# Batch 29 of a graph layer: exponentials kept in the PSUM banks of the distances, and masked from there

## Chip, core and metric

The kernel runs on one core of a Trainium2 chip. The metric is the device time of one execution in microseconds (us), and the time of a kernel is the median over several executions. A profile is one further execution, recorded instruction by instruction. Its span runs from the first to the last instruction. Engines are named as in the profile: PE (TensorE, matrix products), PEld (its weight loads), DVE (VectorE), ACT (ScalarE), POOL (GpSimd) and SP (SyncE, which issues most transfers here).

## What is computed

The input is `x` (32 batches of 512 nodes with 256 features, fp32) and `adj` (32 masks of 512 x 512, fp32 zeros and ones). After a layer norm and a relu, which give the `x` below, the layer computes for each batch:

```python
xc = transpose(x)
h = relu(bn1(conv1(xc)));  h = bn2(conv2(h, 17 taps))
x_conv = transpose(relu(h + xc))
s = x @ w_se.T + b_se                    # 3 numbers per node
sq = sum(s * s, axis=-1)
dist = sq[:, :, None] + sq[:, None, :] - 2.0 * einsum('bnd,bmd->bnm', s, s)
A = exp(-dist) * mask                    # 512 x 512 for each batch
msg = relu(x @ w_msg.T + b_msg)
x_nmp = einsum('bnm,bmd->bnd', A, msg)
# then a gated unit on [x_conv, x_nmp] and x; its output is added to the input
```

The change touches the line that forms `A`, for one batch of the 32.

## The kernel before

**Stages.** The 32 batches are worked in two groups of 16 (`GB`). For each group, `first_part` normalises, runs conv1 and takes the data to a frequency form, in which conv2 is a set of small products. Then `nodes` runs over the 16 batches of the group; it does the frequency products (`product`) and, batch by batch, distances, exponentials, mask and the sum over neighbours. After both groups a last phase goes through the 16 pairs of batches: `inverse` takes conv2 back, `gates_rz` and `gate_n` form the gates, `finish` stores the result. Every phase issues its instructions in an order written out by hand; each engine works through its own in that order and waits only for semaphores.

**The node loop.** For group 1 the order of batches is 31, 30, 16, 17, ..., 29, so batch 29 = `B - 3` is the last one. The loop works one batch ahead: while it sums batch `b` over its neighbours, it prepares the next, `more[0]`. The steps for a batch are

- `factors` (L467): two transposes on PE of the small feature tables give `SL` and `SR`;
- `turn` (L479): DVE turns 128 x 512 pieces of the mask into the tile `at`, of which there are two buffers;
- `exponents` (L486): four products `pd` (L493) put the negated distances of 128 nodes against 512 into four PSUM banks, then four ACTIVATEs on ACT (L495) write their exponentials into the SBUF tile `A` (two buffers);
- `masked` (L497): DVE multiplies each quarter of `A` by its piece of the mask (L499), in place;
- `aggregate` (L526) or, for most batches, `aggregate7` (L538): PE sums over the neighbours.

`aggregate` makes two results of 128 x 512 (L532), one for each half of the 256 features. Each is a chain of four products, over the four quarters of `A` in order. A product in fp32 shows in the trace as two MATMUL instructions, so a result is eight of them. ACT copies each result out of its bank (L534), and `save_nmp` (L571) stores both halves.

**The end of the second loop.** With `last` = 13, the 15th and the 16th batch (28 and 29) go through `aggregate`, and there are no frequency products left to put between. The order on PE is then: first half of batch 28, the distances of batch 29, second half of batch 28, both halves of batch 29. On DVE it is: `turn` of the quarters 0 and 1, `masked` of 0 and 1, `turn` of 2 and 3, `masked` of 2 and 3.

**What comes next.** The last phase starts on other engines before this is over. POOL loads the operands of the first pair and the combined weights, and forms the differences that the gates need (`sums`, L649; L653 in the trace, on the tiles `hp`, `np`, `cp`), four for each tile. PE goes on with `inverse` of pair 0 (L663, banks `pc`), whose result DVE and ACT turn into `cp` (L667, L669), and then the gates (`into`, L675).

**Banks.** There are eight PSUM banks, and all that needs one takes the next in turn: `bank(name)` (L105) asks a pool with eight buffers and one tag. A bank asked for comes free when everything that reads its earlier tenant is done.

Of the kernel before, what the change touches and what calls it, by code (L numbers as in the profile page):

```python
# [12 lines left out]
AF = mybir.ActivationFunctionType  # L13
# [52 lines left out]
def gnn_layer(  # L66
# [15 lines left out]
    nc = tc.nc  # L82
    B, N, D = x.shape
# [21 lines left out]
    def bank(name):  # L105
        return psum.tile([P, N], FP, tag="bank", name=name)

    X, ADJ, XN, HT, HQ, H1, MSG, A, NMP, ST, SL, SR = ({} for _ in range(12))
    XP, HP, NP, CP, YT, RZ, NT, OUT, AT, TS, MS = ({} for _ in range(11))
# [376 lines left out]
    def exponents(b):  # L486

        A[b] = pools["nodes"].tile([P, NC, N], FP, tag="A", name=f"A_{b}", bufs=2)
        sl, sr = SL.pop(b), SR.pop(b)
        pd = [bank(f"pd_{b}_{mc}") for mc in range(NC)]  # L490
        for mc in range(NC):
            rows = slice(32 * mc, 32 * mc + 3 * NS)
            nc.tensor.matmul(pd[mc], sl[rows, :], sr[rows, :], start=True, stop=True)  # L493
        for mc in range(NC):
            nc.scalar.activation(A[b][:, mc, :], pd[mc], AF.Exp)  # L495

    def masked(b, mcs):  # L497
        for mc in mcs:
            nc.vector.tensor_mul(A[b][:, mc, :], A[b][:, mc, :], AT.pop((b, mc)))  # L499

    H = N // 2

    def quads(t, width):
        return [t[:, 2 * k : 2 * k + 2, width * j : width * (j + 1)] for k in range(2) for j in range(2)]

    def affinity_sums(b):
        b11, b12, b21, b22 = quads(A[b], H)
        t = TS[b] = pools["seven"].tile([P, 3, 2, H], FP, tag="ts", name=f"ts_{b}", bufs=1)
        sub = ALU.subtract
        return [partial(nc.gpsimd.tensor_tensor, dst, x, y, op=sub)  # L510
                for dst, x, y in ((t[:, 0], b22, b12), (b12, b12, b11), (t[:, 1], b22, b12), (t[:, 2], b21, t[:, 1]))]
# [26 lines left out]
    def aggregate7(b):  # L538

        m11, s1, m12, m22 = quads(MSG.pop(b), P)  # L540
        b11, t1, b21, b22 = quads(A.pop(b), H)
        (s3, s2, s4), (t3, t2, t4) = ([t[:, n] for n in range(3)] for t in (MS.pop(b), TS.pop(b)))
        nmp = NMP[b] = work.tile([P, DC, N], FP, tag="nmp", name=f"nmp_{b}", bufs=1)
        c11, c12, c21, c22 = (nmp[:, i, H * j : H * (j + 1)] for i in range(2) for j in range(2))
        p1 = pools["seven"].tile([P, H], FP, tag="p7", name=f"p7_{b}", bufs=3)

        def add_product(bk, left, right, first):
            for k in range(2):
                nc.tensor.matmul(bk, left[:, k, :], right[:, k, :], start=(first and k == 0), stop=(k == 1),  # L549
                                 skip_group_check=True)  # L550

        x, y, z = (bank(f"pn{k}_{b}")[:, :H] for k in range(3))
        add_product(x, m11, b11, True)
# [457 lines left out]
    with tc.tile_pool(name="freq", bufs=1) as fpool:  # L1011
# [33 lines left out]
        def nodes(g, xf, units, last, following=()):  # L1045
# [35 lines left out]
            message(todo[1], [1])  # L1081
            features(todo[1])
            exponents(todo[0])
            turn(todo[0], [0, 1])
            masked(todo[0], [0, 1])
            turn(todo[0], [2, 3])
            masked(todo[0], [2, 3])
            prepare(pw, g, units[1], xf)
            for step in affinity_sums(todo[0]):
                step()  # L1090
            for i, b in enumerate(todo):
# [36 lines left out]
                if more:  # L1128
                    turn(more[0], [0, 1])
                    exponents(more[0])  # L1130
                    masked(more[0], [0, 1])
# [122 lines left out]
```

## Time and profile before

| | |
|---|---|
| median of four runs | 1807.76 us (1806.5 to 1809.77) |
| the profiled execution | 1805.22 us |
| its span | 1803.1 us |
| mean granted clock of TensorE | 0.999 |

The stages in the profiled execution, with the busy time of the engines in each (us):

| from : to | length | PE | DVE | ACT | POOL |
|---|---|---|---|---|---|
| 0 : 164, first part of group 0 | 164.00 | 159.14 | 122.53 | 90.67 | 54.39 |
| 164 : 420, node loop of group 0 | 256.00 | 255.73 | 207.07 | 131.02 | 201.93 |
| 420 : 556, first part of group 1 | 136.00 | 135.93 | 107.14 | 57.94 | 60.16 |
| 556 : 808, node loop of group 1 | 252.00 | 251.82 | 193.53 | 124.85 | 193.10 |
| 808 : 823.6, its end, up to the distances of batch 29 | 15.60 | 15.60 | 10.82 | 6.85 | 8.86 |
| 823.6 : 837.7, batch 29 | 14.10 | 12.03 | 7.78 | 3.82 | 12.99 |
| 837.7 : 1803.1, inverse and gates | 965.40 | 956.54 | 564.81 | 220.54 | 258.44 |

The bounds of the stages are put by hand where the work changes. Matmuls overlap, so the busy time of PE is the time in which at least one is under way.

How to read the lines below: a line of a timeline has the start and the duration in us, the engine, the line of the kernel, the operation, the tiles (what is written <- what is read, buffer numbers left out), the size, how many instructions are merged, and in brackets the idle time of the engine before them and what ended it. A line of the chain of waits has start, duration, engine, tile, line and count: it is followed back from the last instruction, at each step to whatever released it or to the instruction before it on its engine.

### The profile page before, as it was taken

What the parts mean: (1) busy time and instruction counts of PE and PEld (TensorE: products, weight loads), DVE (VectorE), ACT (ScalarE), POOL (GpSimd) and SP (SyncE); (2) the same over time, 40 slices, a digit from 0 to 9 for tenths busy, and PEclk for the clock granted to TensorE, in tenths of its full rate; (3) what the DMA queues carried; (4) which work ended last, traced back from release to release, by engine and by line L of the source; (5) the groups of instructions that cost most, each with busy time, mean ns of one, the idle gap of its engine ahead of it and who ended that gap; (6) DMA issues with size and microseconds to landing.
All of it is one profiled execution on the core that took longest, in us unless ns stands there. A gap on an engine that the chain in (4) does not pass through costs nothing.

```text
span 1803.1 us, 21211 instructions
## 1 busy us (share of the span) xinstructions
PE 1786.8 (99%) x6974; PEld 1148.4 (64%) x6974; DVE 1213.7 (67%) x2242; ACT 635.7 (35%) x1348; POOL 789.9 (44%) x733
## 2 busy tenths in 40 slices
PE   8999999999999999999999999999999999999998
PEld 6677888888998888885554555455545554555444
DVE  7885877887986777874356645665566556655666
ACT  4556555453345445443221222122212221222121
POOL 3432887877344878786123132313321332133221
PEclk9999999999999999999999999999999999999999
DMA  9999989876769889889043234323442344124402
GB/s 257 310 300 227 244 235 237 225 214 212 236 222 232 237 227 230 237 211 313 1 123 102 46 97 123 108 48 91 123 114 52 80 123 119 59 68 123 122 19 52
DMA packets 307089, 288.27 MB, mean 160 GB/s; under 512 B 146764, under 2 KB 237420, under 8 KB 306596
## 3 DMA queue, kind: packets, MB, share of 16 engines
q1 hardware_dynamic: 296948, 261.44, 53.6%
q0 software_dynamic: 6592, 23.50, 4.2%
q10 hardware_dynamic: 3440, 1.97, 0.4%
q8 instruction: 56, 0.92, 0.2%
q14 instruction: 53, 0.43, 0.1%
HBM read 190.45 MB, written 96.40 MB: 159 GB/s over the span
## 4 chain that ended last, share of the span: by engine, by line
PE 95%; DVE 2%; issue 1%; POOL 1%; DMA 1%; ACT 0%; SPq 0%; ACTq 0%; DVEq 0%; POOLq 0%
PE pg L675 30%; PE pn L675 15%; PE py L400 12%; PE pn L549 10%; PE pm L451 6%; PE pc L336 6%; PE pc L663 5%; PE px L351 4%; PE pd L493 2%; PE pw L260 2%; PE phT L316 1%; PE pz L675 1%; PE psr L475 1%; PE pn L532 0%; DMA w2p<-in_w2T_dram 0%
## 5 line engine op out<-in xcount | busy, mean ns | idle before, releaser
L653 POOL TENSOR_TENSOR hp<-hp 128x512 f32<-128x512 f32 x64 | 81.3, 1281 | 413.2 <-DMA hp<-hd 381.8
L675 PE MATMUL pg<-hp,sw 128*128 128x512 f32 x434 | 221.8, 593 | 0.7 <-DVE rz L694 0.5
L675 PE MATMUL pg<-np,sw 128*128 128x512 f32 x434 | 221.6, 592 | 0.0
L675 PE MATMUL pg<-cp,sw 128*128 128x512 f32 x434 | 221.6, 592 | 0.0
L653 POOL TENSOR_TENSOR cp<-cp 128x512 f32<-128x512 f32 x64 | 80.6, 1269 | 229.6 <-ACT cp L669 228.4
L690 ACT ACTIVATE rz<-rz,brz 128x512 f32<-128x512 f32 x93 | 67.0, 721 | 260.2 <-DVE rz L694 260.2
L367 POOL TENSOR_TENSOR wsum<-wt 128x512 f32<-128x512 f32 x78 | 111.3, 1428 | 103.7 <-DMA wt<-wd 64.7
L400 PE MATMUL py<-wt,xf 128*128 128x256 f32 x640 | 154.2, 384 | 0.0
L675 PEld LDWEIGHTS pg<-hp,sw 128*128 128x128 f32 x434 | 82.2, 190 | 104.7 <-issue 97.1
L675 PEld LDWEIGHTS pg<-cp,sw 128*128 128x128 f32 x434 | 82.5, 190 | 103.8 <-issue 103.8
L675 PEld LDWEIGHTS pg<-np,sw 128*128 128x128 f32 x434 | 82.5, 190 | 103.8 <-issue 103.8
L499 DVE TENSOR_TENSOR A<-A,at 128x512 f32<-128x512 f32 x128 | 138.7, 1122 | 5.4 <-ACT A L495 5.2
L400 PEld LDWEIGHTS py<-wt,xf 128*128 128x128 f32 x640 | 117.1, 190 | 34.9 <-issue 19.7
L814 ACT ACTIVATE nt<-nt,vech 128x512 f32<-128x512 f32 x64 | 46.2, 722 | 236.2 <-DVE nt L813 236.2
L336 PE MATMUL pc<-w,hT 128*128 128x256 f32 x512 | 118.1, 383 | 0.8 <-DVE hT L320 0.8
L451 PE MATMUL pm<-wmsg,hq 128*128 128x259 f32 x512 | 117.5, 381 | 0.0
L675 PE MATMUL pn<-np,sw 128*128 128x512 f32 x224 | 114.4, 592 | 0.0
L675 PE MATMUL pn<-cp,sw 128*128 128x512 f32 x224 | 114.4, 592 | 0.0
L675 PE MATMUL pn<-hp,sw 128*128 128x512 f32 x224 | 114.4, 592 | 0.0
L336 PEld LDWEIGHTS pc<-w,hT 128*128 128x128 f32 x512 | 94.6, 190 | 24.2 <-issue 6.4
L451 PEld LDWEIGHTS pm<-wmsg,hq 128*128 128x128 f32 x512 | 96.5, 189 | 14.7
L663 PEld LDWEIGHTS pc<-back,yt 128*128 128x128 f32 x640 | 92.7, 190 | 7.7 <-issue 7.7
(173 smaller groups left out, 3371.8 us busy)
## 6 DMA issues: line engine op xcount, KB each, us to landing
wt<-wd SPq DMA_DIRECT2D x80, 512.0 KB, 7.4
adj<-in_adj_dram SPq DMA_DIRECT2D x128, 256.0 KB, 6.6
wd<-wst SPq DMA_DIRECT2D x64, 320.0 KB, 5.8
yd<-y SPq DMA_DIRECT2D x76, 256.0 KB, 5.2
yt<-yd SPq DMA_DIRECT2D x30, 640.0 KB, 6.5
hd<-hT SPq DMA_DIRECT2D x32, 512.0 KB, 4.9
nd<-nmp SPq DMA_DIRECT2D x32, 512.0 KB, 3.0
xb<-in_x_dram SPq DMA_DIRECT2D x128, 128.0 KB, 3.7
```

Source lines behind the costliest of these rows:

```text
L336: nc.tensor.matmul(p[:, j, :], HT[b][:, ic, c * P : (c + 1) * P], w1[:, ic, :], start=(ic == 0), stop=(ic == DC - 1))
L351: nc.tensor.matmul(p[:, j * 2 * L : (j + 1) * 2 * L], H1[b][:, c0 + j, ic * P : (ic + 1) * P], fwd, start=True, stop=True)
L367: nc.gpsimd.tensor_tensor(t, WT[g, u][:, 0], WT[g, u][:, 1], op=ALU.add)
L400: nc.tensor.matmul(dst, v[:, ic, :], w[:, ic, :], start=(ic == 0), stop=(ic == DC - 1))
L451: nc.tensor.matmul(p[:, : D + NS], hq[:, ic, c * P : (c + 1) * P], wmsg[:, ic, :], start=(ic == 0), stop=(ic == DC - 1))
L499: nc.vector.tensor_mul(A[b][:, mc, :], A[b][:, mc, :], AT.pop((b, mc)))
L549: nc.tensor.matmul(bk, left[:, k, :], right[:, k, :], start=(first and k == 0), stop=(k == 1), skip_group_check=True)
L653: nc.gpsimd.tensor_tensor(t[:, dst, :], t[:, a, :], t[:, b, :], op=sub)
L663: nc.tensor.matmul(bk[:, t0:t1], YT[p][j][:, c, oc * P : (oc + 1) * P], back[:, n : n + t1 - t0], start=(c == 0), stop=(c == len(spans) - ...
L675: nc.tensor.matmul(bk[:, t], sw[:, k, q, o, :], terms[k][q][:, t], start=(first and i == 0), stop=(i == len(ks) - 1), skip_group_check=True)
L690: nc.scalar.activation(rz[:, g, j, :], src, AF.Sigmoid, bias=brz[:, g : g + 1], scale=1.0)
L814: nc.scalar.activation(n, n, AF.Tanh, bias=b_in[:, i : i + 1], scale=1.0)
```

## The change

For the batches listed in `in_banks` the ACTIVATE writes the exponentials back into the bank that it reads, in place of a quarter of `A`; the list holds batch 29 alone. A table `EXP` keeps for each quarter where the exponentials are, and `masked` reads them from there. The product with the mask is written to `A` as before, so `aggregate` is unchanged. For all other batches the same instructions are issued as before.

```diff
@@ exponents(b)
         for mc in range(NC):
-            nc.scalar.activation(A[b][:, mc, :], pd[mc], AF.Exp)
+            if b in in_banks:
+                EXP[b, mc] = pd[mc]
+            else:
+                EXP[b, mc] = A[b][:, mc, :]
+            nc.scalar.activation(EXP[b, mc], pd[mc], AF.Exp)
 
     def masked(b, mcs):
         for mc in mcs:
-            nc.vector.tensor_mul(A[b][:, mc, :], A[b][:, mc, :], AT.pop((b, mc)))
+            nc.vector.tensor_mul(A[b][:, mc, :], EXP.pop((b, mc)), AT.pop((b, mc)))
 
     H = N // 2
+    EXP = {}
+    in_banks = (B - 3,)
```

## The prediction

> **What bounds the kernel now.** I read the page first: its busy shares and its chain.
>
> ```profile
> PE 1786.8 (99%) x6974; PEld 1148.4 (64%) x6974; DVE 1213.7 (67%) x2242; ACT 635.7 (35%) x1348; POOL 789.9 (44%) x733
> ...
> PE 95%; DVE 2%; issue 1%; POOL 1%; DMA 1%; ACT 0%; SPq 0%; ACTq 0%; DVEq 0%; POOLq 0%
> ```
>
> TensorE (PE) is at work almost throughout and is 95% of the chain that ended last. A change to four exponentials and four mask products therefore counts only where PE waits for them. So the second view is the chain of waits in the stretch from 819 to 845 us, where the last batch (batch 29) is made and used:
>
> ```profile
> 824.84 2.07 ACT A L495 x4
> ...
> 826.95 1.75 DVE A L499
> 828.70 0.68 DVE at L482 x2
> ...
> 830.42 2.84 DVE A L499
> ...
> 833.31 4.56 PE pn L532 x10
> 837.87 5.65 PE pc L663 x40
> ```
>
> Here, for once, the chain leaves PE: exponentials, masks, transposes, masks, and only then matmuls. The timeline of the same stretch gives the durations (start, duration, engine, line, count, then idle time before and what ended it):
>
> ```profile
> 823.86 5.98 POOL L653 TENSOR_TENSOR hp<-hp 128x512 f32<-128x512 f32 x4
> 824.69 5.42 PE L532 MATMUL pn<-A,msg 128*128 128x512 f32 x12
> 825.47 3.24 DVE L499 TENSOR_TENSOR A<-A,at 128x512 f32<-128x512 f32 x2 [4.09 <-ACT A L495]
> 828.63 1.29 DVE L482 STREAM_TRANSPOSE at<-adj 128x512 f32<-128x512 f32 x2
> 829.85 3.40 DVE L499 TENSOR_TENSOR A<-A,at 128x512 f32<-128x512 f32 x2
> 830.55 1.13 PE L532 MATMUL pn<-A,msg 128*128 128x512 f32 x2 [0.44 <-DVE A L499]
> 831.42 5.52 POOL L653 TENSOR_TENSOR np<-np 128x512 f32<-128x512 f32 x4
> 833.31 4.56 PE L532 MATMUL pn<-A,msg 128*128 128x512 f32 x10 [1.64 <-DVE A L499]
> 837.70 1.57 PE L663 MATMUL pc<-back,yt 128*128 128x136 f32 x10
> ```
>
> PE stands still twice, each time for a mask product. The four products take 1.56, 1.75, 0.64 and 2.83 us (starts 825.47, 826.95, 829.85, 830.42), while GpSimd (POOL) runs the subtractions of the next phase. In the whole trace only here do matmuls wait for L499.
>
> **What the two stops cost.** Matmuls of this form start 0.429 us apart (eight from 820.09 take 3.60 us; one lasts 0.592, so (3.60 - 0.592)/7 = 0.43). The group of twelve has its last start at 830.11 - 0.592 = 829.52. Twelve more follow (2 and 10), then L663. Without a stop L663 would start 13 x 0.429 = 5.58 us later, at 835.09; it starts at 837.70. The stops cost **2.61 us**: 0.60 and 1.80 of waiting, and twice 0.105 because the first matmul after each lasts 0.697.
>
> **The change, part by part.** Counts stay: four ACTIVATEs and four products for batch 29, no DMA, and nothing for the other 31 batches.
>
> *Exponentials (L495).* They read a bank as before and write the same bank, not A. No row shows ScalarE writing a bank. Successive ones start 0.48 us apart now (2.06 us for four, one is 0.594). The nearest rows on both sides: copies out of a bank (L534), 0.586, and sigmoids from SBUF to SBUF (L690), 0.722. I take 0.594, nearest because the input and the function are the same. [...]
>
> *Mask products (L499).* One input now comes from a bank. Rows with a bank first and SBUF second, in this same node loop and beside the same busy POOL:
>
> ```profile
> L454 DVE TENSOR_TENSOR msg<-pm,bmsg x128: 407/415/425, 158.0 to 812.3; 128x256 f32<-128x256 f32 x128
> ...
> L499 DVE TENSOR_TENSOR A<-A,at x128: 642/1210/2832, 167.4 to 830.4; 128x512 f32<-128x512 f32 x128
> ```
>
> (minimum, median, maximum in ns). With both inputs in SBUF the time spreads over a factor of four; with one in a bank 128 instructions stay within 18 ns. At the full width of 512 the rows with a bank are L706, 0.678 to 0.689 (two of them inside POOL's subtractions of 848.99 to 855.40), L694, 0.688, and L667, 0.751. So a product from a bank takes 0.64 (the fastest product now) to 0.75; I take 0.69, the same operation. The four fall from 6.79 to 2.76 us. [...]
>
> *New order in time.* Durations added end to end, though VectorE overlaps them a little: first product 825.47 to 826.16, second to 826.85, two transposes of 0.70 to 828.25, third to 828.94, fourth to 829.63. Undisturbed, PE asks for the first at 828.23, the second at 829.09, the third at 829.95 and the fourth at 830.80. The margins of the last two are 1.0 and 1.2 us. With every term at its upper bound (exponentials 0.72 apart, products 0.75) the third ends at 829.3 and the fourth at 830.0, still 0.7 early. Both stops go: **-2.61 us**; the product that now ends at 828.70, 0.4 ahead of its matmul, holds nothing up.
>
> *What waits move.* ScalarE no longer waits for A's old buffer; VectorE's first product does, but its last readers (the L549 matmuls) were done by 819.71, 5.8 us earlier. Behind that product stand only transposes and products of the same batch. The four banks stay taken until the products are read, some 0.7 to 3 us longer. Eight banks go round, so the next users are the second to fourth bank of the inverse and the first of the gates, the earliest at 839.1 - 2.6 = 836.5, 7 us after the last product. Cost nothing; uncovered it would be those 3 us.
>
> *What is late next.* After 837.70 PE runs on into L663 and L675. The gates' POOL operands (L653 cp) wait for ScalarE behind L663's banks, and so move along; POOL is free for them from about 837, and they start at 843.72 - 2.61 = 841.1. POOL's subtractions lose their stretches too (1.59 and 1.72 beside 1.27), about 0.8 us that stays on POOL. Transfers only start earlier. From 838 to the end the wait list names 0.7 us of PE waiting (for L694 and L706), so the gain is passed to the end. PE itself can gain no more than 2.61 + 0.7 = 3.3 us.
>
> **The sum.** The profiled execution took 1805.22 us with a span of 1803.1. Less 2.61: span 1800.5, execution 1802.6. That execution was 2.54 below the median of the four runs (1807.76; 1806.5 to 1809.77), so the forecast for the median is 1807.76 - 2.61 = **1805.15 us**, 0.14% faster. A measurement here can tell about 0.2%, 3.6 us, from no change, so the forecast counts as within it.
>
> **Rivals.**
> 1. *The products stay slow* (9%): they are long for another reason than two SBUF inputs beside POOL, and no PE time comes back: 1807.76. For it: the fourth starts 1.0 us before POOL's np subtraction. Against: L454, L706.
> 2. *Half of it* (6%): the first stop goes, 0.71 us, but the fourth product still runs into POOL and keeps its 1.90 us: 1807.05. For it: only the fourth is so long. Against: the same rows, and its start would be at 829, between POOL's two groups.
> 3. *Slower: writing into the bank being read is expensive on ScalarE* (5%). No row shows it. Up to (830.80 - 0.69 - 824.84)/4 = 1.3 us per exponential it is hidden; it decides against the change from (833.25 - 0.69 - 824.84)/4 = 1.93 us, four times today's spacing. At 3.0 us the fourth product ends at 824.84 + 12 + 0.69 = 837.5, 4.3 later than now: 1812.0.
>
> **How the numbers follow.** The likeliest, 80%, is 1805.15, by itself 1805.0 to 1805.4. The four runs lie from 1.3 below to 2.0 above their median, and a median of a few moves by about 0.9. Low end: most gain, 1807.76 - 3.3, less 0.9, about 1803.5. High end: 1807.05 of rival 2 with part of that scatter, 1807.6; beyond stay rival 3, half of rival 1 and the tails. Faster by over 0.2% (under 1804.14) needs the forecast with a favourable scatter of 1.0: 17% in all. Slower: rival 3 and a tail of rival 1: 6%. Within: 77%.
>
> **What would show it.** In the changed profile the four products read pd and at, 0.64 to 0.75 us each; L532 has no wait on L499; its matmuls after 824.69 run as one group of 24; L663 starts at 835.1; exponentials stay near 0.6 us. Products still over 1 us would prove rival 1 or 2 right, exponentials over 1.3 us rival 3. A later start of L675's first cp operand than 841.1 on POOL, or new PE waits after 838, would show a gain given back, and make the prediction wrong.

## The result, and the profile after

| | before | after |
|---|---|---|
| median | 1806.56 us (54 runs, 1804.44 to 1809.77) | 1803.12 us (36 runs, 1800.49 to 1808.25) |
| ratio, 95% interval | | 0.9982 [0.9977, 0.9987] |
| span of the profiled execution | 1803.1 us | 1801.0 us |

The change makes the kernel 0.18% faster, 3.25 us by the ratio (2.3 to 4.2 by its interval). The forecast was 0.14%, 2.61 us, and a median of 1805.15 us within 1803.5 to 1807.6. The measured median lies 0.4 us below that range.

The timeline of the profile after, in the stretch in which batch 29 is made and used (start, duration, engine, line, tiles, count, idle time before):

```profile
825.25 10.57 PE L538 MATMUL pn<-A,msg 128*128 128x512 f32 x24
835.66 0.57 PE L669 MATMUL pc<-back,yt 128*128 128x136 f32 x3
...
826.01 1.29 DVE L503 TENSOR_TENSOR A<-pd,at 128x512 f32<-128x512 f32 x2 [4.07 <-ACT pd L499]
827.22 1.30 DVE L482 STREAM_TRANSPOSE at<-adj 128x512 f32<-128x512 f32 x2
828.44 1.25 DVE L503 TENSOR_TENSOR A<-pd,at 128x512 f32<-128x512 f32 x2
...
824.41 5.21 POOL L659 TENSOR_TENSOR hp<-hp 128x512 f32<-128x512 f32 x4
829.56 1.61 POOL L623 DMA_DIRECT2D sw<-ws  x3
831.19 5.19 POOL L659 TENSOR_TENSOR np<-np 128x512 f32<-128x512 f32 x4
...
825.34 2.05 ACT L499 ACTIVATE pd<-pd 128x512 f32<-128x512 f32 x4 [0.47 <-PE pd L493]
```

The three groups of matmuls of before (12, 2 and 10, with two stops between) are one group of 24. The two pairs of products take 1.29 and 1.25 us where they took 3.24 and 3.40, although POOL is at the same work beside them. The exponentials take no longer. POOL's hp subtractions also lose their stretch: 5.21 us against 5.98.

The single durations, from the instructions of two lines (minimum/median/maximum in ns):

```profile
L503 DVE TENSOR_TENSOR A<-A,at x124: 641/1212/1775, 168.2 to 817.8; 128x512 f32<-128x512 f32 x124
...
L503 DVE TENSOR_TENSOR A<-pd,at x4: 653/678/692, 826.0 to 829.0; 128x512 f32<-128x512 f32 x4
...
L499 ACT ACTIVATE A<-pd x124: 581/593/625, 166.9 to 815.6; 128x512 f32<-128x512 f32 x124
...
L499 ACT ACTIVATE pd<-pd x4: 578/587/605, 825.3 to 826.8; 128x512 f32<-128x512 f32 x4
```

The 124 products that still read two tiles in SBUF go from 0.64 to 1.78 us; the four from banks stay within 39 ns.

And the chain of waits, which no longer leaves PE (compare 824.84 to 833.31 in the chain of before):

```profile
824.25 1.07 PE pd L493 x8
825.33 10.50 PE pn L538 x24
835.82 5.65 PE pc L669 x40
```

**A yardstick.** Executions of one kernel differ among themselves by 5 us (before) and 8 us (after), so single traces are compared by one stretch: from the first distance product of batch 29 (823.62 before, 824.18 after) to the first matmul of the inverse (837.70 and 835.66). It is 14.08 us before and 11.48 after: **2.60 us less**. From there to the end of the span it is 965.4 us in both.

### The profile page after: what moved, and what is told of

Its sections match the earlier page's. It is cut to its first block, busy times and chain, and to the rows that moved or that the text cites. A ratio compares the mean times of both kernels' runs of the same rounds, so it can differ in the third digit from the quotient of the medians.

```text
span 1801.0 us, 21211 instructions
## 1 busy us (share of the span) xinstructions
PE 1786.8 (99%) x6974; PEld 1150.4 (64%) x6974; DVE 1216.8 (68%) x2242; ACT 635.2 (35%) x1348; POOL 791.2 (44%) x733
## 3 DMA queue, kind: packets, MB, share of 16 engines
q10 hardware_dynamic: 3440, 1.97, 0.4%
## 4 chain that ended last, share of the span: by engine, by line
PE 95%; DVE 1%; issue 1%; DMA 1%; POOL 1%; ACT 0%; ACTq 0%; SPq 0%; DVEq 0%; POOLq 0%
PE pg L681 30%; PE pn L681 15%; PE py L400 12%; PE pn L555 10%; PE pm L451 6%; PE pc L336 6%; PE pc L669 5%; PE px L351 4%; PE pd L493 2%; PE pw L260 2%; PE phT L316 1%; PE pz L681 1%; PE pn L538 1%; PE psr L475 1%; DMA w2p<-in_w2T_dram 0%
```

## The experiments

In the table, ratios are to runs of the kernel before made beside them on the same chip.

| run | ratio, 95% interval | stretch, us | products 0 to 3, us |
|---|---|---|---|
| before (first profile) | | 14.08 | 1.56, 1.75, 0.64, 2.83 |
| after (first profile) | 0.9982 [0.9977, 0.9987] | 11.48 | 0.69, 0.68, 0.65, 0.67 |
| before once more | 0.9998 [0.9989, 1.0007] | 14.06 | 1.55, 1.75, 0.64, 2.83 |
| after once more | 0.9981 [0.9972, 0.9990] | 11.47 | 0.69, 0.68, 0.65, 0.67 |
| POOL held back | 0.9988 [0.9979, 0.9996] | 11.47 | 0.69, 0.68, 0.65, 0.68 |
| mask in banks | 0.9985 [0.9977, 0.9994] | 12.27 | 0.69, 0.68, 0.67, 0.67 |
| quarters 0, 1 only | 0.9981 [0.9972, 0.9991] | 12.11 | 0.69, 0.68, 1.74, 1.75 |
| quarters 2, 3 only | 0.9978 [0.9968, 0.9988] | 12.18 | 1.56, 1.75, 0.65, 0.67 |
| loads after np | one execution | 14.11 | 1.56, 1.75, 1.76, 1.75 |
| loads beside products 2, 3 and four repeats | one execution | 13.10 | 0.69, 0.68, 0.68, 0.69 |
| five products more | one execution | 13.71 | 0.68, 0.68, 0.65, 0.67 |
| nine products more | one execution | 17.64 | 0.68, 0.68, 0.65, 0.68 |
| all batches in banks | 0.9994 [0.9985, 1.0003] | 11.48 | 0.69, 0.68, 0.65, 0.67 |
| all but batch 14 | 0.9984 [0.9972, 0.9996] | 11.48 | 0.69, 0.68, 0.65, 0.67 |

### Is POOL what makes the products long?

The kernel before, with one column copied on DVE after the last product and read by POOL before its subtractions, which therefore start later:

```diff
 def masked(b, mcs):
     ...
+    if b == B - 3 and NC - 1 in mcs:
+        nc.vector.tensor_copy(held[:, :1], A[b][:, NC - 1, :1])
 ...
+nc.gpsimd.tensor_copy(held[:, 1:], held[:, :1])
 sums(HP[0], True)
```

> The kernel before, exponentials and products in A as ever; only POOL's subtractions hp and np of the next phase start after the fourth product (a one-column copy on DVE, read by a one-column copy on POOL). Theory (the products are long because POOL works beside them): the four take 0.64 to 0.69 us each, PE's two stops vanish, 2.6 us faster than before, POOL ends its np subtractions near 842 instead of 837, which nobody waits for. Rival (they are long because of the tile A or of what ScalarE does): the products of 1.6 to 2.8 us stay, no gain.

Its timeline:

```profile
827.66 1.29 DVE L499 TENSOR_TENSOR A<-A,at 128x512 f32<-128x512 f32 x2 [4.09 <-ACT A L495]
828.87 1.30 DVE L482 STREAM_TRANSPOSE at<-adj 128x512 f32<-128x512 f32 x2
830.10 1.25 DVE L499 TENSOR_TENSOR A<-A,at 128x512 f32<-128x512 f32 x2
...
831.75 5.16 POOL L656 TENSOR_TENSOR hp<-hp 128x512 f32<-128x512 f32 x4
...
826.88 10.57 PE L535 MATMUL pn<-A,msg 128*128 128x512 f32 x24
```

Exponentials and products stay in `A`, and the products are as short as from banks (0.65 to 0.69 us); PE's matmuls are one group of 24. So it is POOL's work beside them that makes products with two SBUF inputs long (up to 2.83 us in the kernel before), and nothing in `A` or on ScalarE. POOL ended its np subtractions later, as forecast, and only 0.4 us of new PE waiting shows, near the end of the gates (0.59 where 0.22 was). Holding the other engine back does nearly what the change does.

### Does it matter which input lies in a bank?

The kernel before; for batch 29 the mask is turned into banks and the exponentials stay in `A`:

```diff
-    at = AT[b, mc] = pools["nodes"].tile([P, N], FP, tag="at", ...)
+    at = AT[b, mc] = (bank(f"pat_{b}_{mc}") if b == B - 3 else
+                      pools["nodes"].tile([P, N], FP, tag="at", ...))
```

> The kernel before, but for batch 29 DVE turns the mask into four banks instead of the tile at; the exponentials stay in A. ScalarE writes no bank. Theory (one input of the product in a bank is what counts, whichever): products 0.64 to 0.69 us, both stops gone, 2.6 us faster than before, like the change. Rival (ScalarE's write to the bank is what helps): products stay at 1.6 to 2.8 us, no gain.

```profile
824.79 1.29 DVE L500 TENSOR_TENSOR A<-A,pat 128x512 f32<-128x512 f32 x2 [4.07 <-ACT A L496]
825.99 1.31 DVE L483 STREAM_TRANSPOSE pat<-adj 128x512 f32<-128x512 f32 x2
827.22 1.26 DVE L500 TENSOR_TENSOR A<-A,pat 128x512 f32<-128x512 f32 x2
...
824.81 10.57 PE L533 MATMUL pn<-A,msg 128*128 128x512 f32 x24 [0.73 <-ACT A L496]
```

The products (lines 1 and 3) are short, 0.67 to 0.69 us, although ScalarE writes no bank: one input in a bank is enough, and it may be either. The stretch is 0.8 us longer than with the change (1.8 us gained, where 2.6 were expected) because the eight banks now run short: PE waits 0.73 us, and the profile names an exponential that still reads a bank. Of the two ways the change takes the one that needs no more banks.

### Which of the four products count?

The change with `if b in in_banks and mc in (0, 1)`, and with `mc in (2, 3)`:

> The change for quarters 0 and 1 of batch 29 alone; quarters 2 and 3 go through A as before. Measured by the stretch from the first distance product of batch 29 to the first matmul of the inverse: 14.08 us before, 11.48 with the change. Theory (a product from SBUF is long only where POOL works beside it): products 0 and 1 take 0.69, product 2 starts about 1.6 us earlier than before and meets the end of POOL's hp subtractions, product 3 falls between POOL's two groups; stretch 11.5 to 12.1, 2.0 to 2.6 us faster than before. Rival (each quarter's own product decides): the last product keeps its 2.8 us, stretch above 13.

> The change for quarters 2 and 3 alone. Theory: products 0 and 1 stay at 1.6 to 1.75 us, so product 2 starts as late as before and the first stop of PE stays (0.60 and 0.10 us); product 3 takes 0.68 and the second stop goes; stretch 12.2, 1.9 us faster than before. Rival: the early products are of no matter, stretch 11.5.

Quarters 0 and 1 alone:

```profile
825.48 1.29 DVE L503 TENSOR_TENSOR A<-pd,at 128x512 f32<-128x512 f32 x2 [4.07 <-ACT pd L499]
...
827.90 3.41 DVE L503 TENSOR_TENSOR A<-A,at 128x512 f32<-128x512 f32 x2
...
831.37 4.56 PE L538 MATMUL pn<-A,msg 128*128 128x512 f32 x10 [0.37 <-DVE A L503]
```

Quarters 2 and 3 alone:

```profile
826.90 3.24 DVE L503 TENSOR_TENSOR A<-A,at 128x512 f32<-128x512 f32 x2 [4.09 <-ACT A L499]
...
831.28 1.24 DVE L503 TENSOR_TENSOR A<-pd,at 128x512 f32<-128x512 f32 x2
...
831.98 5.42 PE L538 MATMUL pn<-A,msg 128*128 128x512 f32 x12 [0.44 <-DVE A L503]
```

Each half brings most of it (1.97 and 1.90 us of 2.60), which looks odd only if one adds them. The products and the transposes between stand in one line on DVE. With the first two short, the last two start 2 us earlier and may be long (1.74 and 1.75) with only the last one late, which stops PE for 0.37 us. With the last two short, they start as late as before, so the first stop stays, and the second goes. In the first run a detail of the expectation was wrong. Product 3 did start between POOL's groups of subtractions (at 829.56; hp ended at 829.09, np began at 830.67), but it took 1.75 us all the same, the first 1.1 of them with nothing on POOL but the issue of three loads:

```profile
829.04 1.61 POOL L623 DMA_DIRECT2D sw<-ws  x3
830.67 5.68 POOL L659 TENSOR_TENSOR np<-np 128x512 f32<-128x512 f32 x4
```

That wait comes up again below.

### How much slack is there?

The change, with n more products of the same kind in front of product 0, n = 5 and 9 (they are written to a quarter of `A` that is overwritten later):

```diff
+    if b in in_banks and 0 in mcs:
+        for _ in range(5):
+            nc.vector.tensor_mul(A[b][:, NC - 1, :], EXP[b, 0], AT[b, 0])
```

> The change, with five more products of the same kind (from bank 0, written to a quarter of A that is overwritten later) in front of the first product of batch 29: about 0.61 us each, 3.05 us on DVE. Theory (PE's matmuls wait for the end of each product and for nothing else): product 0 ends 1.0 us after PE asks for it, product 2 another 0.5 late; PE stops for 1.5 to 1.9 us in all, stretch 13.0 to 13.4. Rival (the order of things on DVE has more slack, or PE is held by something else): stretch stays near 11.5.

> As with five more products in front, but nine, 0.725 us apart: product 0 ends 2.9 us later than with five, so PE stops for about 4.3 us before its first matmul of batch 29. Theory (a stop of 2 us or more lowers the granted clock for some 3 us, as in the run with all batches in banks): the eight matmuls after it start up to 0.86 us apart instead of 0.43, clock about 0.5 there, and the stretch is 16.5 to 18.5 us. Rival (the low clock there had another cause): clock 1.0, matmuls 0.43 apart, stretch about 15.9 us.

With five: the added products started 0.725 us apart, not 0.61, so the stretch came out longer than the 13.0 to 13.4 expected. Each of them writes the same place as the one before, which may be why; that was not tested. The matmul that needs product 0 started 1.46 us late and the one that needs product 2 another 0.57. With the first matmul after each stop, which lasts 0.1 us longer, that is 2.24, the measured 13.71 - 11.47. So the delays of these two products account for all that PE lost.

With nine, the windows around the stop (stretch, its length, busy time of PE, PEld, DVE, ACT and POOL with counts, then granted clock, DMA share and GB/s):

```profile
830.00:833.50 3.50, 0.00 (x0) 0.00 (x0) 3.36 (x7) 0.00 (x0) 3.40 (x6) 1.00 0.83 223
833.50:837.50 4.00, 3.92 (x6) 1.63 (x7) 3.01 (x6) 0.00 (x0) 3.21 (x3) 0.59 0.96 379
837.50:842.00 4.50, 4.50 (x12) 2.11 (x11) 0.00 (x0) 0.58 (x1) 0.00 (x0) 0.99 0.95 391
```

A stop of 4.20 us is followed by four microseconds with a granted clock of 0.59 on average, in which matmuls start up to 0.85 us apart. The stretch is 17.64 us, where 4.20 us of stop alone would give an estimated 15.8 (11.47, the stop, and 0.1 for the first matmul after it).

### The rest of the loops: all batches in banks

`in_banks = range(B)`, and then `[b for b in range(B) if b != GB - 2]`, all but batch 14:

> The change applied to all 32 batches. Theory: all 128 products take about 0.68 us, DVE's busy time falls by about 57 us (97 products of 1.27 to 0.68), POOL's a little; PE waits for products nowhere else, so the time is that of the change within 0.5 us. Rival 1: four banks held longer in every batch make PE wait for banks: slower than the change, perhaps than before. Rival 2: freer DVE and POOL bring some further microseconds.

> The change for all batches but 14, the second of the first loop, whose products wait for its mask to land and whose banks the sums of batch 15 asked for next. Theory (holding the banks cost only there, 2.0 us of stop and 1.7 us of matmuls at half clock after it): the loop from the first message product of group 0 to that of group 1 takes 391 to 392 us as before (396.7 with all batches); time as with the change, 0.9975 to 0.999 of the kernel before. Rival (banks are missed in many batches): the loop stays above 394 us.

All 128 products took 0.65 to 0.69 us and DVE's busy time fell by 66 us (1213.7 to 1147.9), where 57 were expected. No time came of that. The waits of PE outside batch 29 are not for products, so there was nothing to gain; and one loss came in, at the second batch of the first loop:

```profile
175.80 1.68 PE L555 MATMUL pn<-A,msg 128*128 128x256 f32 x7
179.46 1.89 PE L555 MATMUL pn<-ts,ms 128*128 128x256 f32 x4 [1.99 <-DVE A L503]
181.15 1.91 PE L555 MATMUL pn<-A,msg 128*128 128x256 f32 x4
182.85 1.12 PE L555 MATMUL pn<-ts,ms 128*128 128x256 f32 x4
```

The sums of batch 15 ask for a bank that holds exponentials of batch 14, whose products wait for a mask that lands at 177.4 (it lands as late in the kernel before, at 177.9, where no bank hangs on it). After the stop of 1.99 us PE's next eight matmuls start 0.42 us apart where they start 0.215 apart before, and the windows show why:

```profile
177.40:179.40 2.00, 0.07 (x1) 0.00 (x0) 1.96 (x4) 0.37 (x1) 0.74 (x2) 1.00 1.22 215
179.40:183.00 3.60, 3.54 (x9) 2.82 (x10) 3.60 (x8) 0.37 (x1) 1.85 (x2) 0.53 1.27 192
```

The granted clock is 0.53 over 3.6 us. From the first matmul of these sums to the next transposes (L470) it takes 9.96 us (175.58 to 185.54), in the kernel before 6.04 (176.40 to 182.44): stop and low clock cost 3.92 us. From the first message product of group 0 to that of group 1 the trace with all batches takes 396.7 us, before 391.3. Without batch 14 it is 392.7, 0.7 above what was expected at most: the stop and the slow matmuls are gone, and the ratio is that of the change again (0.9984). The last 1.1 us of it, two short waits of PE near 450 us for DVE and POOL, were also there with all batches, and their cause was not followed up. In the twelve other profiles, which issue the same instructions there, this loop takes 390.6 to 392.4 us. One trace is not the average, though: by the medians of executions on the same chip, the kernel with all batches in banks is 2.7 us slower than the change (1805.35 against 1802.65), as its first rival had it, while its trace loses 5.4 us in this loop. Neither version beats the change.

### What blocks a product for 2.8 us?

The fourth product took 2.83 us in both traces of the kernel before; in the fourteen traces no other exceeds 1.82. It began 1.0 us before POOL's np subtractions, while POOL was issuing three loads. Two runs look at these loads: the kernel before with `load_combined(sw, 2, 7)` behind `sums(NP[0], False)`, and one in which the loads alone lie beside the products.

> The kernel before, but POOL's three loads of the combined weights 2 to 6 are issued after its np subtractions, not between hp and np; products stay in A. In the kernel before, the one product of 2.83 us lay beside these loads and np; no other product exceeds 1.77 us. If POOL's subtractions alone block a product: products 2 and 3 overlap np at once and take 1.3 to 1.8 us each, or one of them 2.8 again. If the issuing of loads is what blocked it: no product over 1.8 us, and PE's stops shrink to 2 us or less.

> The kernel before with POOL's work rearranged: its three loads of weights 2 to 6 are issued when the last mask piece of batch 29 has been turned, beside products 2 and 3 and four repeats of product 3 (the mask is 0 and 1, a repeat changes nothing); the subtractions come after all of these. If issuing loads holds up a product with two SBUF inputs: at least one of the six takes over 1 us. If only subtractions do: all six take 0.64 to 0.72 us.

With the loads moved away products 2 and 3, beside np, took 1.76 and 1.75:

```profile
830.43 3.43 DVE L499 TENSOR_TENSOR A<-A,at 128x512 f32<-128x512 f32 x2
...
830.38 5.83 POOL L653 TENSOR_TENSOR np<-np 128x512 f32<-128x512 f32 x4
```

In the other run six products (two, and four repeats) took 0.68 to 0.69 each. The loads were issued from 831.07 to 832.66, so product 3 and the first two repeats (830.99 to 833.12) lay beside them, and the other three products before or after:

```profile
831.07 1.59 POOL L625 DMA_DIRECT2D sw<-ws  x3
...
830.39 4.19 DVE L504 TENSOR_TENSOR A<-A,at 128x512 f32<-128x512 f32 x6
```

So loads alone do not hold up a product, and subtractions alone made it 1.76 us. Products waited while loads were issued only where subtractions came before and after them: product 3 of the kernel before, and product 3 in the run with quarters 0 and 1 in banks. Product 2 of the kernel before stood there too, beside the first load, and took 0.64. Why the one waits and not the other is open. PE lost the same with the loads moved (stretch 14.11), since two products of 1.75 end about as late as 0.64 and 2.83.

### Is the measured gain larger than the traces show?

> The changed kernel once more, beside fresh runs of the kernel before on the same chip. Theory: all of the gain is the two stops of PE, 2.61 us, so the ratio lies near 0.9986. Rival: the first comparison's 0.9982 (about 3.3 us) holds 0.6 us that the trace of one execution does not show; then 0.9982 comes back. The level of both kernels may differ from the first runs by about 1 us, the difference less.

> The kernel before against itself. Comparisons so far put the kernels without PE's stops 2.2 to 4.0 us ahead, while their traces save 1.8 to 2.6 us. Theory (scatter of single executions): ratio 1.000, within 0.9992 to 1.0008. Rival (whatever is compared with the kernel before looks about 0.7 us faster): ratio near 0.9996, and the excess over 2.61 us is no effect of the change. If the ratio is 1.000 with a narrow interval, the excess of 0.6 us stays open.

Once more the change came out at 0.9981, as the rival had it, and the kernel before against itself at 0.9998 [0.9989, 1.0007]: the comparison itself favours nobody by more than its interval, which holds the 0.9996 of the rival as well. The 2.60 us of the traces (0.9986) lie within both intervals of the change, and 0.6 us of excess is less than either can tell. The kernels that shorten PE's stops came out at 0.9978 to 0.9988, apart from the one with all batches, which adds a stop. For quarters 2 and 3 alone, the 1.90 us of the trace would be 0.9989, just outside the interval.

A part of the excess lies where no trace looks. An execution of the kernel before is longer than its span by 2.10 us on average (33 executions), one of the changed kernel by 1.86 (11 on the same chip). All kernels with the four exponentials of batch 29 in banks have 1.81 to 1.91, all others, those with two of the four among them, 2.08 to 2.12. So some 0.24 us of the gain are outside the span; why is open. For the rest no trace shows where more would come from.

## Why the prediction failed on the time and held on the mechanism

**The bound** was right: PE lost time to products of batch 29 twice, 2.61 us in all. The stretch lost 2.60.

**The products** were put at 0.69 (bounds 0.64 and 0.75) and take 0.65 to 0.69. The reason given, two SBUF inputs beside a working POOL, is shown by the run with POOL held back and by the one with the mask in banks. A source in a bank costs no time of its own here: with POOL held back the four products take 0.69, 0.68, 0.65 and 0.68 us from SBUF, with the change 0.69, 0.68, 0.65 and 0.67 from banks.

**The exponentials** were put at 0.594 as before; written into the bank they take 0.589 on average, 13 ns less than the 0.602 into `A` in the kernel before (the mean of the four of batch 29 each). Rival 3, an expensive write to the bank that is read, is out.

**The margins** of the last two products were put at 1.0 and 1.2 us. In the profile after, product 2 ends at 829.09 and its matmul starts at 830.51; product 3 ends at 829.69, its matmul starts at 831.37: 1.4 and 1.7 us. The sum laid durations end to end, and DVE overlaps them by some 0.1 us each.

**What is late next**: nothing, as said. POOL's first cp subtraction starts at 841.68; measured from the stretch's start (824.18, where it was 823.62) that is 2.60 earlier. The wait list after 843 us names the same 0.7 us of PE.

**The step that failed is the level**, "the forecast for the median is 1807.76 - 2.61", together with "a median of a few moves by about 0.9". The median of before came out at 1806.56 over 54 runs, 1.20 below the four runs that the forecast stood on; that alone, less 2.61, would have been 1803.95, inside the range. The other 0.83 of the miss of 2.03 is the difference of the two medians (3.44) less 2.61. Of this, 0.23 is a second term of the sum that was mis-sized: "span 1800.5, execution 1802.6" takes the 2.1 us outside the span as fixed, and the changed kernel has 1.87. The remaining 0.6 no run could tell from scatter. The low end allowed for a gain of 3.3 and a level lower by 0.9; both were a little short. The prediction had the warning in hand and used it only to report it: the profiled execution, 1805.22, lay below all four timed ones. With five executions from 1805.2 to 1809.8, a level of 1807.76 was not known to 0.9, and the low end should have allowed for one 1 to 2 us lower.

**Where the scatter comes from** can in part be seen in the traces. The first message product of group 0 starts between 156.5 and 162.3 us in the fourteen profiles, whose kernels are the same up to there. PE's wait for a transfer near 14 us (L260) differs, 0.4 us in the first profile of before and 2.2 in the first of the change. And in six of the fourteen the granted clock is 0.50 for 3.41 or 6.83 us, somewhere between 16 and 24 us or between 74 and 83 (from 17.17 to 20.58 in the first profile of the change); their mean clocks are 0.995 to 0.998. The two latest starts, 161.1 and 162.3, are those of the two profiles with 6.83 us of it after 74 us. The timed executions point the same way: of 78 of the kernel before, the 35 with a mean clock of 0.999 have spans of 1804.1 us on average, the ten with 0.997 have 1805.9. After the node loop the profiles agree within 0.4 us (965.4 to 965.8 from the inverse to the end). A change of 2.6 us is lost in a single span, and plain in a stretch.

The rivals: products that stay slow (1) and half of it (2) are out by the durations and by the single group of 24. Within 0.2% was the likeliest class, and 0.18% is within it, but only just: the interval runs from 0.13 to 0.23%, so that this came true was partly luck.

## What to carry to other kernels

Where a product of two SBUF tiles on VectorE ran beside GpSimd's own tile work and stretched (up to 2.83 us), leaving either input in the PSUM bank where it was made kept it at its undisturbed time (0.65 to 0.69 us); so did holding GpSimd back (0.65 to 0.69). It is worth anything only where the engine that sets the end waits for that product: for one batch of 32 it was 2.6 us, for the other 31 nothing, and held banks cost 3.9 us in the one trace in which a late mask kept them. Compare a small change by the stretch that it touches, not by the span.

## What was not expected of the hardware

The granted clock fell after some stops of PE and not after others. After stops of 1.30 us (five products more) and 1.64 (the kernel before) it stayed at 1.00 and matmuls kept their spacing of 0.43 us. After 1.99 us it was 0.53 over 3.6 us, after 4.20 us 0.59 over 4.0, so that a stop of 1.99 us cost 3.9. The length of the stop does not decide alone: in the profile with quarters 2 and 3 in banks a stop of 1.30 us that ended at 14.78 was followed by a clock of 0.50 from 16.28 to 19.69, and in the second profile of the change the clock was 0.50 from 16.31 to 19.72, although PE was busy for 3.00 of the 3.41 us before. Every stretch of 0.50 in the fourteen traces, but for one at the very end of each, lasts 3.41 us or twice that. What decides is open.
